# A depthwise convolution on TensorE and one product fewer on GpSimd, in a four-layer float32 network

## The chip, the cores and the metric

The kernel runs on one core of one Trainium2 chip, as one program. The metric is the device time of one execution in microseconds. The five engines are called here as in the profile: PE (TensorE, matrix products), DVE (VectorE), ACT (ScalarE), POOL or GpSimd, and SP, which issues most of the transfers. PSUM is the memory that PE writes its products to; DVE and ACT read it too; GpSimd works on SBUF alone in this kernel.

## What is computed

Four layers act on a tensor x of 8 samples, 384 channels and 32 x 32 pixels, in float32. The first and the third are state-space layers, the second a deformable convolution, the fourth a shift of channels by small separable kernels. The change is in the first, whose core is this (L = 1024 tokens, 768 inner channels, 16 states):

```python
x = x + mamba(group_norm(x))          # layer 0, on tokens
xz = xseq @ in_proj_w.T;  xin, z = split(xz)
xc = depthwise_conv(xin, conv_w, width 3, causal) + conv_b
u  = silu(xc)
dt, B, C = split(u @ x_proj_w.T);  dt = softplus(dt @ dt_proj_w.T + dt_proj_b)
h[t] = exp(dt[t] * A) * h[t-1] + dt[t] * u[t] * B[t]     # for each of 16 states
y[t] = sum over states of h[t] * C[t]  + u[t] * D
out  = (y * silu(z)) @ out_proj_w.T
```

The convolution of a channel is `w2*x[t] + w1*x[t-1] + w0*x[t-2] + b`.

## The kernel before

**Tiling.** `ssm_layer` is called for layer 0 and layer 2 with the same code and a few switches (`mlp` is true for layer 2). A sample's 1024 tokens are cut into two halves of 512 (`h` 0 and 1). One half of one sample is a *step*: 16 steps per layer, even ones first halves, odd ones second halves. The 768 inner channels are six groups `j` (or `d`) of 128. Within a group, the 128 channels x 16 states are laid out as eight *units* `m`, each a tile of 128 partitions x 2 x 512. So a step is 48 units, and one unit is:

- `inputs` (L502, GpSimd): `db = dub * B`, 128 x 1024, issued three units ahead;
- `decays` (L494, ACT): `da = exp(dtb * A)` in two operations, into PSUM, two units ahead; `da` has two buffers (`da0`, `da1`);
- `scan` (L514, DVE): the recurrence over 512 tokens, 128 x 1024;
- `with_c` (L525 on GpSimd, or L527 on DVE): the product with C, into `hs`, a ring of seven buffers;
- `keep_last` (L520, ACT), in first halves, and `add_carry` (L487, GpSimd) in second halves, which hand the state from one half to the next.

Every four units `read_out` (L537, PE) sums four `hs` tiles over the states into `y`. Which units have their product with C on GpSimd is told by `GP_C`: in layer 0 units 0, 2, 4, 6 of the even groups and 0, 2, 5 of the odd ones. For these the scan writes to `hs` itself; for the others it writes over `da`, and DVE makes the product right after it.

**Order.** Within the layer the order of each engine is written out by hand. `plan` puts all the rest of the work at unit numbers t (0 to 47) of a step, into one queue for each of ACT, DVE, GpSimd and PE. At unit t the loop does, in this order: ACT's queue for t, `scan`, `with_c` if it is DVE's, `keep_last`, `decays` of unit t+2, DVE's queue, `inputs` of unit t+3, `with_c` if it is GpSimd's, GpSimd's queue, PE's queue, `read_out`. Each engine executes its own instructions in the order in which they are issued.

The work of a step that is planned around the 48 units belongs to the step before (output projection), to the step itself (gate: z projection L546 on PE, then SiLU L550 on ACT between two table loads; softplus of dt, L408 to L451, for the group two ahead) and to the step after. For the step after, `inner` (L348) makes the input projection `ps_in` of group d at units `TI` = 15, 16, 17, 24, 25, 26 on PE, three products of 128 x 128 by 128 x 512 each; each float32 product is two PE instructions in the trace.

**The convolution before.** One unit after `inner`, `conv_last` (L352, ACT) writes `u = w2 * ps_in + b` to SBUF. In first halves it also copies the last two columns to `halo` (L354); in second halves it adds the two tokens that come from the half before, with three operations on single columns (L360). Two units after `inner`, `conv` (L368, DVE) adds the other two taps straight from PSUM, in two operations. Later SiLU runs over three groups at a time (L374). The first step's convolutions stand in a prologue that runs all groups in a row before the units begin.

PSUM tiles of PE's products (`ps_in`, `ps_dt`, `ps_sp`, `ps_z`, `ps_o`, `ps_x`) share three buffers; a new one takes a buffer whose readers are done.

Of the kernel before, what the change touches and what calls it, by code (L numbers as in the profile page):

```python
# [8 lines left out]
F32 = mybir.dt.float32  # L9
AF = mybir.ActivationFunctionType  # L10
ALU = mybir.AluOpType
# [4 lines left out]
P = 128  # L16
# [6 lines left out]
ND = DI // P  # L23
# [3 lines left out]
TS = L // 2  # L27
# [4 lines left out]
IP = P // NI  # L32
NSUB = P // IP
NQP = NS // NI // 2
GP_C = {0: ((0, 2, 4, 6), (0, 2, 5)), 2: ((0, 2, 5), (0, 2, 5))}
PE_SUM = (0,)
ENGINES = {mybir.EngineType.Activation, mybir.EngineType.PE, mybir.EngineType.DVE, mybir.EngineType.Pool}
FF = 4 * C
# [40 lines left out]
V_CW, V_CB, V_DB, V_D, V_A = 0, 18, 24, 30, 36  # L79
# [17 lines left out]
class Net:  # L97
# [107 lines left out]
    def ssm_layer(self, li, src, dst, shift=None):  # L205
        tc, nc, ins = self.tc, self.nc, self.ins
        mlp = li == 2
        gp_c = GP_C[li]
        pe_sum = li in PE_SUM
        sel = self.cols[:, Q_SEL : Q_SEL + IP]  # L210
        with ExitStack() as ctx:
            wp = ctx.enter_context(tc.tile_pool(name=f"w{li}", bufs=1))
# [11 lines left out]
            vec = wp.tile([P, ins[f"vec{li}"].shape[1]], F32, name="vec")  # L224
# [5 lines left out]
            if mlp:  # L230
                w1_d = ins["w1"].rearrange("(k p) o -> p k o", p=P)
                w2_d = ins["w2"].rearrange("(k p) o -> p k o", p=P)
                mean_w = wp.tile([P, P], F32, name="mean_w")
                nc.vector.memset(mean_w, 1.0 / C)
            else:
                win = wp.tile([P, G, 2 * DI], F32, name="win")
                nc.sync.dma_start(out=win, in_=win_d)
                wout = wp.tile([P, ND, C], F32, name="wout")
                nc.sync.dma_start(out=wout, in_=wout_d)
                diag_d = wp.tile([P, ND, P], F32, name="diag_d")  # L240
                for j in range(ND):
                    nc.gpsimd.tensor_scalar(
                        diag_d[:, j, :], self.ident, vec[:, V_D + j : V_D + j + 1], None, ALU.mult
                    )
            nc.sync.dma_start(out=wx, in_=ins[f"wx{li}"].rearrange("(k p) o -> p k o", p=P))
            nc.sync.dma_start(out=wdt, in_=ins[f"wdt{li}"])

# [8 lines left out]
            def v(i):  # L256
                return vec[:, i : i + 1]

            def fetch_in(s, o):
                if not mlp:  # L260
                    s["win", o] = win[:, :, o * P : (o + 1) * P]
                    return
                t = s["win", o] = p2.tile([P, G, P], F32, name="winr", tag="winr", bufs=3)
                nc.sync.dma_start(out=t, in_=win_d[:, :, o * P : (o + 1) * P])
# [75 lines left out]
            def inner(s, d):  # L340
                if d == 0:
                    s["u"] = p2.tile([P, ND, TS], F32, name="u", tag="u")
                    if s["h"] == 0:
                        s["sib"]["halo"] = p2.tile([P, ND, 2], F32, name="halo")
                xn, w = s["xn"], s["win", d]
                s["in", d] = ps = self.psum("ps_in")
                for k in range(G):
                    nc.tensor.matmul(ps, w[:, k, :], xn[:, k, :], start=(k == 0), stop=(k == G - 1))  # L348

            def conv_last(s, d):  # L350
                ps, ud = s["in", d], s["u"][:, d, :]
                nc.scalar.activation(ud, ps, AF.Identity, bias=v(V_CB + d), scale=v(V_CW + 3 * d + 2))  # L352
                if s["h"] == 0:
                    nc.scalar.copy(s["sib"]["halo"][:, d, :], ps[:, TS - 2 : TS])  # L354
                else:

                    halo = s["halo"][:, d, :]
                    for i, k, wi in ((0, 0, 0), (0, 1, 1), (1, 1, 0)):
                        c = ud[:, i : i + 1]
                        nc.scalar.activation(  # L360
                            c, halo[:, k : k + 1], AF.Identity, bias=c, scale=v(V_CW + 3 * d + wi)
                        )

            def conv(s, d):
                ps, ud = s["in", d], s["u"][:, d, :]
                w0, w1 = v(V_CW + 3 * d), v(V_CW + 3 * d + 1)
                for i, wi in ((1, w1), (2, w0)):
                    nc.vector.scalar_tensor_tensor(  # L368
                        ud[:, i:], ps[:, : TS - i], wi, ud[:, i:], ALU.mult, ALU.add
                    )  # L370
# [133 lines left out]
            def hs_tile(s, m):  # L504
                t = s["hs", m] = p2.tile([P, 2, TS], F32, name="hs", tag="hs", bufs=7)
                return t

            def scan(s, j, m):
                if j == 0 and m == 0 and s["h"] == 0:
                    s["sib"]["st"] = p2.tile([P, ND, NS], F32, name="st")  # L510
                da, db = s["da", m], s["db", m]
                h = hs_tile(s, m) if m in gp_c[j % 2] else da
                h1, da1, db1 = (t.rearrange("p i l -> p (i l)") for t in (h, da, db))
                nc.vector.tensor_tensor_scan(h1, da1, db1, 0.0, ALU.mult, ALU.add)  # L514
                s["h", m] = h
# [5 lines left out]

            def with_c(s, j, m):
                c = s["bc"][m // NSUB][:, 1]
                if m in gp_c[j % 2]:
                    nc.gpsimd.tensor_tensor(s["hs", m], s["hs", m], c, ALU.mult)  # L525
                else:
                    nc.vector.tensor_tensor(hs_tile(s, m), s["da", m], c, ALU.mult)  # L527
# [127 lines left out]
            def plan(prev, s, nxt):  # L655
                act, dve, pool, pe = queues = [[[] for _ in range(T + NU)] for _ in range(4)]

                def put(q, t, fn, *args):
                    if not args or args[0]:
                        q[t].append((fn, *args))  # L660

                for j in range(ND):
                    t = NU * j
# [6 lines left out]
                    n, k = (s, j + 2) if j + 2 < ND else (nxt, j + 2 - ND)  # L670
# [36 lines left out]
                for d, t in enumerate(TI):  # L707
                    put(pe, t - 2, fetch_in, nxt, d)
                    put(pe, t, inner, nxt, d)
                    put(act, t + 1, conv_last, nxt, d)  # L710
                    put(dve, t + 2, conv, nxt, d)
                put(pe, 32 if mlp else 30, x_proj, nxt, 0, ND // 2)
                put(pe, 33 if mlp else 32, x_proj, nxt, ND // 2, ND)
                put(act, 34 if mlp else 33, x_store, nxt)
# [32 lines left out]
            with tc.manual_schedule(engines=ENGINES):  # L747
                s = steps[0]
# [9 lines left out]
                for d in range(ND):  # L758
                    fetch_in(s, d)
                    inner(s, d)  # L760
                    conv_last(s, d)
                    conv(s, d)
                    if d == ND - 2:
                        silu(s, 0, ND // 2)
                x_proj(s, 0, ND // 2)
# [19 lines left out]
                for i, (s, j, m) in enumerate(units):  # L785
                    c, t = divmod(i, T)
                    if t == 0:
                        queues = plan(
                            steps[c - 1] if c else None, s, steps[c + 1] if c + 1 < len(steps) else None
                        )  # L790
                        for k, q in enumerate(over or ()):
                            for i0, items in enumerate(q):
                                queues[k][i0][:0] = items
                        act, dve, pool, pe = queues
                        over = [q[T:] for q in queues]
                    mine = m in gp_c[j % 2]
                    run(act[t])
                    scan(s, j, m)
                    if not mine:
                        with_c(s, j, m)  # L800
                    keep_last(s, j, m)
                    ahead = units[i + 2] if i + 2 < len(units) else (None, None, None)
                    if ahead[2] == 0:
                        first_token(*ahead[:2])
                    if ahead[0]:
                        decays(*ahead)
                    run(dve[t])
                    if i + 3 < len(units):
                        inputs(*units[i + 3])
                        if ahead[2] == 0:  # L810
                            carry(*ahead[:2])
                            add_carry(*ahead)
                        if units[i + 3][2] > 0:
                            add_carry(*units[i + 3])
                    if mine:
                        with_c(s, j, m)
                    run(pool[t])
                    run(pe[t])
                    for r in late.pop(i, ()):
                        read_out(*r)  # L820
                    if m % NSUB == NSUB - 1:
                        late.setdefault(i + (1 if m == NU - 1 else 2), []).append((s, j, m // NSUB))
# [1113 lines left out]
```

## Time and profile before

| | us |
|---|---|
| median of 3 runs | 9294.69 (9293.85 to 9295.26) |
| the profiled execution | 9297.33, span 9295.5 |
| layer 0: first to last scan, 16 steps | 75.5 to 2879.5 |
| an even step of layer 0 / an odd one | 172.1 / 179.5 |
| layers 1 / 2 and 3 | about 2900 to 5750 / from there to the end |

Mean durations in layer 0:

| operation | engine, line | us |
|---|---|---|
| scan, 128 x 1024 | DVE L514 | 2.29 |
| product with C, 128 x 1024 | DVE L527 / POOL L525 | 1.225 / 2.356 |
| `db`, 128 x 1024 | POOL L502 | 2.355 |
| decay, 128 x 512 | ACT L494 | 0.691 |
| `conv_last`, 128 x 512 | ACT L352 | 0.764 |
| single column | ACT L360 | 0.382 |
| tap of the convolution, 128 x 511 | DVE L368 | 0.745 |
| table load | ACT L550, L377 | 1.283 |

How to read the profile. A line of the *timeline* has the start in us from the first instruction, the duration in us, the engine, the source line, the operation, `out<-in`, sizes and the number of merged instructions; in brackets stands the idle time of the engine before it and what ended it by the profile. A line of the *groups* has the busy time in us, the mean in ns of one, and after the bar the idle time ahead of the group. A wait for several things is put down to one of them, and not always to the one that ended last. PE's matrix products overlap, so their durations are longer than their spacing. The clock column is the share of full speed that PE was granted.

### The profile page before, as it was taken

The page shows a single profiled execution, that of the slowest core. Times are in us where ns is not written, and L with a number is a line of the kernel's source. Part 1 is how long each engine was busy: PE and PEld are TensorE (multiplying, and loading weights), DVE is VectorE, ACT ScalarE, POOL GpSimd, SP SyncE. Part 2 cuts the span into 40 slices and gives each one's busy share as a digit, 9 for nine tenths or more (in the row PEclk, how much of TensorE's full clock was granted, in tenths as well). Part 3 has the DMA queues.
Part 4 walks back from the last instruction along what each step waited for, and adds up shares of the span by engine and source line. Part 5 has one row for each costly group of instructions (what it writes and reads, how often), then busy time and mean ns, then how long its engine had stood idle before and what let it go on. Part 6 is the DMA issues. An engine that isn't in the chain of part 4 may idle for free. (4 is left out here: it accounts for less than half of the span.)

```text
span 9295.5 us, 93074 instructions
## 1 busy us (share of the span) xinstructions
PE 7557.6 (81%) x29452; PEld 3856.6 (41%) x29452; DVE 7733.3 (83%) x8617; ACT 6500.3 (70%) x10467; POOL 5645.4 (61%) x3393
## 2 busy tenths in 40 slices
PE   6777677677676999999999997588888888888876
PEld 2222222222223777767777766133333333333333
DVE  6999999999995878878878877788988889898972
ACT  5677677677673878878877876677777677776750
POOL 6999999999994000000000000898989989899964
PEclk7788788788787999999999998798999889999988
DMA  4544544544543333333333333566656666666656
GB/s 123 124 115 113 123 116 114 123 119 114 123 114 81 82 80 85 92 83 85 90 84 86 91 80 85 118 154 151 150 139 155 151 161 147 148 148 145 161 145 112
DMA packets 785233, 1094.47 MB, mean 118 GB/s; under 512 B 274963, under 2 KB 427955, under 8 KB 752985
## 3 DMA queue, kind: packets, MB, share of 16 engines
q1 hardware_dynamic: 722628, 1077.98, 47.6%
q10 hardware_dynamic: 62100, 10.44, 0.7%
q8 instruction: 235, 3.85, 0.2%
q14 instruction: 270, 2.20, 0.1%
HBM read 917.84 MB, written 170.33 MB: 117 GB/s over the span
## 5 line engine op out<-in xcount | busy, mean ns | idle before, releaser
L502 POOL TENSOR_TENSOR db<-dub,bc 128x1024 f32<-128x1024 f32 x1536 | 3603.2, 2355 | 405.9 <-DVE hs L514 224.6
L494 ACT ACTIVATE da<-dtb,vec 128x512 f32<-128x512 f32 x3072 | 2119.5, 691 | 672.9 <-DVE hs L527 416.9
L514 DVE TENSOR_TENSOR_SCAN da<-da,db 128x1024 f32<-128x1024 f32 x912 | 2086.3, 2288 | 258.9 <-ACT da L494 116.4
L435 POOL TENSOR_TENSOR dt<-dt,sp_e 128x512 f32<-128x512 f32 x96 | 122.3, 1274 | 2885.4 <-DMA bc<-bcd 2881.1
L1598 PE MATMUL wacc<-fsm,fxk 128*128 128x221 f32 (+34 forms) x10624 | 1657.2, 315 | 98.1 <-DVE fsm L1568 95.1
L1598 PEld LDWEIGHTS wacc<-fsm,fxk 128*128 128x128 f32 x10624 | 1570.0, 195 | 236.1 <-DVE fsm L1568 159.2
L514 DVE TENSOR_TENSOR_SCAN hs<-da,db 128x1024 f32<-128x1024 f32 x624 | 1423.9, 2282 | 166.4 <-POOL db L487 76.7
L525 POOL TENSOR_TENSOR hs<-hs,bc 128x1024 f32<-128x1024 f32 x624 | 1470.8, 2357 | 15.2 <-ACT st L520 14.9
L1568 DVE TENSOR_TENSOR fsm<-fhy,fhx 128x170 f32<-128x170 f32 (+42 forms) x3216 | 1170.2, 428 | 342.3 <-PE wacc L1598 315.3
L527 DVE TENSOR_TENSOR hs<-da,bc 128x1024 f32<-128x1024 f32 x912 | 1116.9, 1225 | 111.8 <-PE y L537 58.5
L537 PE MATMUL y<-hs,cols 128*32 128x512 f32 x6144 | 826.1, 618 | 160.5 <-POOL hs L525 154.6
L1528 ACT ACTIVATE fhy<-fpyx,cell 128x416 f32<-128x416 f32 (+9 forms) x1280 | 645.5, 576 | 385.0 <-DVE fsm L1568 385.0
L1551 DVE TENSOR_TENSOR fxk<-fxt,fwk 128x1024 f32<-128x1024 f32 (+1 forms) x688 | 787.1, 1179 | 10.2 <-ACT fxt L1330 10.2
L614 PE MATMUL ps_m<-hid,wm 128*128 128x512 f32 x1152 | 550.2, 633 | 61.7 <-ACT hid L609 27.7
L595 PE MATMUL ps_h<-t,wm 128*128 128x512 f32 x1152 | 529.7, 604 | 43.2 <-DVE sp_e L427 25.4
L1533 ACT ACTIVATE fhy<-fhy,cols 128x1344 f32<-128x1344 f32 (+10 forms) x368 | 530.8, 1442 | 12.0
L537 PEld LDWEIGHTS y<-hs,cols 128*32 128x32 f32 x6144 | 171.3, 112 | 798.3 <-issue 497.7
L348 PE MATMUL ps_in<-xn,winr 128*128 128x512 f32 x576 | 328.9, 718 | 174.5 <-ACT xn L337 125.4
L444 PE MATMUL ps_sp<-dt,ident 128*128 128x512 f32 x192 | 168.4, 974 | 290.8 <-ACT dt L414 285.7
L614 PEld LDWEIGHTS ps_m<-hid,wm 128*128 128x128 f32 x1152 | 226.9, 203 | 394.3 <-issue 282.7
L1239 PE MATMUL ps_off<-fxn,fow 128*98 128x465 f32 (+10 forms) x896 | 386.6, 579 | 0.0
L444 PE MATMUL ps_sp<-sp_e,ident 128*128 128x512 f32 x192 | 174.9, 1009 | 259.5 <-DVE sp_e L425 259.5
(212 smaller groups left out, 10436.4 us busy)
## 6 DMA issues: line engine op xcount, KB each, us to landing
dtb<-dtd SPq DMA_DIRECT2D x768, 256.0 KB
dub<-dtd SPq DMA_DIRECT2D x768, 256.0 KB
fpyx<-fposd SPq DMA_DIRECT2D x640, 256.0 KB
wm<-in_w SPq DMA_DIRECT2D x96, 768.0 KB
bc<-bcd SPq DMA_DIRECT2D x256, 256.0 KB
x<-x SPq DMA_DIRECT2D x71, 768.0 KB
dtd<-dt SPq DMA_DIRECT2D x192, 256.0 KB
dtd<-sp_e SPq DMA_DIRECT2D x192, 256.0 KB
```

Of the source, the lines that this page charges most:

```text
L494: nc.scalar.activation(da[:, i, :], s["dtb", j][:, k, :], AF.Exp, scale=na[:, j, n + i : n + i + 1])
L502: nc.gpsimd.tensor_tensor(db, du, s["bc"][p][:, 0], ALU.mult)
L514: nc.vector.tensor_tensor_scan(h1, da1, db1, 0.0, ALU.mult, ALU.add)
L525: nc.gpsimd.tensor_tensor(s["hs", m], s["hs", m], c, ALU.mult)
L527: nc.vector.tensor_tensor(hs_tile(s, m), s["da", m], c, ALU.mult)
L537: nc.tensor.matmul(s["y"][k * IP : (k + 1) * IP, :], sel, s["hs", p * NSUB + k][:, i, :], start=mlp and p == 0 and i == 0, stop=p == NQP - ...
L614: nc.tensor.matmul(ps, s["w2", q][:, f, o * P : (o + 1) * P], s["hid", q][:, f, :], start=(f == 0), stop=(f == 3))
L1528: nc.scalar.activation(hy[:, at : at + (yb - ya) * W], pyx[:, 0, ya * W : yb * W], AF.Abs, bias=bias)
L1533: nc.scalar.activation(hy[:, :at], hy[:, :at], AF.Relu, bias=self.col(Q_ONE), scale=-1.0)
L1551: nc.vector.tensor_tensor(t[:, :n], x, wk[:, j : j + 1, :].to_broadcast([P, n, P]), ALU.mult)
L1568: nc.vector.tensor_tensor(self.sub(sm, at, [(r * w, n), (w, r), (1, w)]), self.sub(hy, hy_at[by] + xa, [(r * W, n), (W, r), (1, w)]), self ...
L1598: nc.tensor.matmul(a[:, ya - 4 * o : yb - 4 * o, xa:xb], k, self.sub(sm, sm_at[by], [(w, yb - ya), (1, w)]), start=False, stop=False,)
```

## The change

Three edits, all for layer 0. `GP_C` is now a list of six groups in both layers, with units 0, 2 and 5 in each; so in layer 0 the even groups give GpSimd three products in place of four, and DVE five in place of four. In a pair of groups GpSimd has six of sixteen products in place of seven. Layer 2 had this pattern before.

The convolution no longer uses DVE. `conv_in` copies the raw `ps_in` to SBUF. `conv_pe` multiplies it on PE by three diagonal matrices, shifted by 0, 1 and 2 columns, into a new PSUM tile `ps_cv`, with two small products for the two edge columns in second halves. `conv_out` adds the bias on the way back to SBUF. The diagonal matrices (18 of 128 x 128) are built once on GpSimd. Layer 2 keeps `conv_last` and `conv`.

```diff
-GP_C = {0: ((0, 2, 4, 6), (0, 2, 5)), 2: ((0, 2, 5), (0, 2, 5))}
+GP_C = {0: ((0, 2, 5),) * 6, 2: ((0, 2, 5),) * 6}
...
+                diag_w = wp.tile([P, 3 * ND, P], F32, name="diag_w")
+                for k in range(3 * ND):
+                    nc.gpsimd.tensor_scalar(
+                        diag_w[:, k, :], self.ident, vec[:, V_CW + k : V_CW + k + 1], None, ALU.mult
+                    )
...
+            def conv_in(s, d):
+                ps, ud = s["in", d], s["u"][:, d, :]
+                nc.scalar.copy(ud, ps)
+                if s["h"] == 0:
+                    nc.scalar.copy(s["sib"]["halo"][:, d, :], ps[:, TS - 2 : TS])
+
+            def conv_pe(s, d):
+                ud = s["u"][:, d, :]
+                s["cv", d] = ps = self.psum("ps_cv")
+                edge = s["h"] == 1
+                nc.tensor.matmul(ps, diag_w[:, 3 * d + 2, :], ud, start=True, stop=False)
+                nc.tensor.matmul(ps[:, 1:], diag_w[:, 3 * d + 1, :], ud[:, : TS - 1], start=False, stop=False)
+                if edge:
+                    halo = s["halo"][:, d, :]
+                    nc.tensor.matmul(ps[:, 0:1], diag_w[:, 3 * d + 1, :], halo[:, 1:2], start=False, stop=False)
+                    nc.tensor.matmul(ps[:, 0:2], diag_w[:, 3 * d, :], halo, start=False, stop=False)
+                nc.tensor.matmul(ps[:, 2:], diag_w[:, 3 * d, :], ud[:, : TS - 2], start=False, stop=True)
+
+            def conv_out(s, d):
+                nc.scalar.activation(s["u"][:, d, :], s["cv", d], AF.Identity, bias=v(V_CB + d))
...
-                h = hs_tile(s, m) if m in gp_c[j % 2] else da
+                h = hs_tile(s, m) if m in gp_c[j] else da
...
-                    put(act, t + 1, conv_last, nxt, d)
-                    put(dve, t + 2, conv, nxt, d)
+                    if mlp:
+                        put(act, t + 1, conv_last, nxt, d)
+                        put(dve, t + 2, conv, nxt, d)
+                    else:
+                        put(act, t + 1, conv_in, nxt, d)
+                        put(pe, t + 1, conv_pe, nxt, d)
+                        put(act, t + 3, conv_out, nxt, d)
...
-                    conv_last(s, d)
-                    conv(s, d)
+                    for fn in (conv_last, conv) if mlp else (conv_in, conv_pe, conv_out):
+                        fn(s, d)
```

The last hunk is the prologue of the first step. The same change of index, from `gp_c[j % 2]` to `gp_c[j]`, is made at two other places.

## The prediction

> **What bounds the kernel now.** The change touches the first state-space layer only, so I read that layer. The page first: five engines, none full over the span. Then the table of stretches, cut at two neighbouring steps of the layer (a step is 48 units, and a unit is one scan). Columns: PE, PEld, DVE, ACT and POOL busy, then granted clock, DMA share, GB/s.
>
> ```profile
> PE 7557.6 (81%) x29452; PEld 3856.6 (41%) x29452; DVE 7733.3 (83%) x8617; ACT 6500.3 (70%) x10467; POOL 5645.4 (61%) x3393
> ```
> ```profile
> 1132.80:1304.90 172.10, 126.54 (x374) 41.46 (x370) 160.13 (x109) 128.27 (x236) 162.11 (x73) 0.81 0.49 118
> 1304.90:1484.40 179.50, 131.04 (x415) 47.39 (x418) 164.44 (x120) 123.31 (x203) 167.33 (x121) 0.81 0.48 118
> ```
>
> The layer is 16 such steps: even ones (first half of a sample) 172.1 us, odd ones 179.5. DVE and GpSimd are both busy some 93% of a step, and PE 73%. The change takes work from the two full engines and gives it to PE, so the question is what DVE waits for in the remaining 7%. The timeline of the even step, DVE, then ACT, then PE, where the convolutions stand:
>
> ```profile
> 1186.84 2.28 DVE L514 TENSOR_TENSOR_SCAN hs<-da,db 128x1024 f32<-128x1024 f32 x1
> 1190.54 2.30 DVE L514 TENSOR_TENSOR_SCAN da<-da,db 128x1024 f32<-128x1024 f32 x1 [1.42 <-POOL db L502]
> ```
> ```profile
> 1186.93 0.60 ACT L550 ACTIVATE sz<-ps_z 128x512 f32<-128x512 f32 x1 [1.60 <-PE ps_z L546]
> 1187.55 1.28 ACT L377 ACT_TABLE_LOAD   x1
> ...
> 1189.04 1.42 ACT L494 ACTIVATE da<-dtb,vec 128x512 f32<-128x512 f32 x2
> 1190.39 0.76 ACT L352 ACTIVATE u<-ps_in,vec 128x512 f32<-128x512 f32 x1
> ```
> ```profile
> 1186.73 5.31 PE L348 MATMUL ps_in<-xn,win 128*128 128x512 f32 x12
> 1191.98 1.93 PE L537 MATMUL y<-hs,cols 128*32 128x512 f32 x16
> 1193.83 2.84 PE L348 MATMUL ps_in<-xn,win 128*128 128x512 f32 x6
> ```
>
> DVE idles 1.42 us before the scan at 1190.54. The row names GpSimd, but the last thing to end before it is ACT's `da` (1189.04 + 1.42 = 1190.46), and ACT was late because its gate waited 1.60 us for PE's `ps_z`. So in this stretch the order is PE, then ACT, then DVE: ACT executes in order, its decays `da` of unit u+2 stand behind whatever the plan put at unit u, and what waits there for PE holds the next scan. One row shows what PE does after a long wait:
>
> ```profile
> 1229.82 5.42 PE L348 MATMUL ps_in<-xn,win 128*128 128x512 f32 x6 [4.75 <-DVE u L368]
> ```
>
> **The parts of the change, each by itself.**
>
> ```profile
> L527 DVE TENSOR_TENSOR hs<-da,bc 128x1024 f32<-128x1024 f32 x432 | 529.1, 1225 | 32.2 <-PE y L537 5.1 <-DVE da L514 0.5
> L368 DVE SCALAR_TENSOR_TENSOR u<-ps_in,vec,u 128x511 f32<-128x511 f32 x192 | 143.0, 745 | 17.4 <-ACT halo L354 14.0
> L525 POOL TENSOR_TENSOR hs<-hs,bc 128x1024 f32<-128x1024 f32 x336 | 791.6, 2356 | 1.2 <-ACT st L520 0.9
> ```
>
> - DVE, per step: 12 `conv` operations go (12 x 0.745 = 8.94 us), three products with C come (3 x 1.225 = 3.68). Net -5.27.
> - GpSimd: three products go, 3 x 2.356 = 7.07 us per step. It hides behind DVE except in odd steps, where `add_carry` (L487) makes it the later one at three or four units.
> - ACT, per convolution: `conv_last` (0.76) becomes a copy (taken as 0.60, from L447's 0.58) and `conv_out` (taken as 0.76, as L352). Where the next step is a second half, three L360 operations of 0.38 go. About even in time; what counts is that ACT now waits twice on PE's queue.
> - PE, per convolution: three float32 products, which the trace before has with `win` as weights, not with a diagonal. A product 128x512 is two instructions; six took 2.84 us in the row at 1193.83 and 5.42 in the row at 1229.82. These are the ends; I take 2.6, the spacing at full clock (2.84 less the drain of the last), since PE is busy just ahead of most convolutions. In even steps, whose successor is a second half, two edge products of one and two columns come on top: nothing at the low end, L145's 18 instructions of 128x2 in 4.00 us at the other, 4 x 0.21 = 0.85, which I take.
> - SP's queue gets no transfer. `spread` of dt and du leaves up to 5 us later where PE's sums come later; its tiles are first used seven units on, some 23 us: nothing.
> - 18 diagonal matrices in the prologue on GpSimd: 18 x 0.58 (`diag_d`: 6 in 3.50 us) = 10.5, finished near 19 us, before the first convolution at 28. Nothing.
>
> **What they do to the path, by hand.** PE's queue now reads in0, conv0, in1, readout, conv1, in2, dt, conv2 and later in3, readout, conv3, in4, dt, conv4, in5, conv5. Each conv waits for ACT's copy of its `in`, and everything behind waits too. I walked the even step with the durations above. An instruction starts when its engine is free and what it reads has ended, in the order of the queues: ACT does, for each unit, first what the plan put there (copies, conv_out, soft_exp, gate), then `keep_last`, then `da` of two units on (1.42). DVE's scan takes 2.2 and a product with C 1.2 from start to start. Zero is 1175.86 us, the start of the scan of unit 13.
>
> | event | before | after |
> |---|---|---|
> | in0 ends (PE) | 13.6 | 13.6 |
> | ACT has taken in0 (behind `da` of 17, 14.6) | 15.3 | 15.15 |
> | conv0: waits 1.6 for that, then 2.6 + 0.85 | - | 18.7 |
> | in1 ends | 16.2 | 21.4 |
> | copy of in1, then `da` of 19 ends (ACT) | 21.1 | 23.5 |
> | scan 19 | 23.9 | 23.5 |
> | readout (1.9) and conv1 (3.45) end | 18.0 | 26.55 |
> | in2 ends | 20.8 | 29.3 |
> | copy of in2, then `da` of 20 ends | 24.3 | 31.5 |
> | scan 20 (DVE was free at 26.95) | 28.8 | 31.5 |
> | scan 21 (behind soft_exp 2.6 and conv_out on ACT) | 31.6 | 36.5 |
> | scan 25 (behind gate and two table loads) | 46.0 | 50.75 |
> | conv3 52.9 to 56.35; in4 ends | 50.8 | 59.1 |
> | in5: behind soft_exp and `conv_out` of conv3, whose PSUM buffer it takes | 59.2 | 67.4 |
> | scan 29 (DVE free at 65.35) | 64.1 | 69.6 |
> | scan 33 | 78.7 | 84.4 |
>
> DVE idles some 13 us more here and works 7.7 us less: the even step is 5.7 us longer. Outside this stretch the extra product of j = 0 and j = 4 (1.2 us) falls into bubbles ahead of units 9 and 41 that ACT's gate makes anyway (1.3 and 1.8 us): nothing.
>
> Odd steps have no edge products. The same walk gives scan 25 at +1.7 and scan 33 at +2.2 us; against it some 2 us of DVE's waits for GpSimd go (list of waits: DVE for L487 43.7 + 35.4 us over eight odd steps, near 10 a step, of which I take only those at units 40 to 46 and 8, since the others sit where ACT is late anyway). Near 0.
>
> Prologue: before, PE runs the 36 `ps_in` instructions without a gap (22.44 to 40.3) and `dbc` is there at 48.1. After, each of six channels is in (2.6), wait for the copy (0.85), conv (2.6) in a row, 6.05 instead of 2.57 us, and the last three go through conv_out and SiLU afterwards: my chain ends at 67.6, +19.5, with nothing beside it.
>
> **Sum:** 8 even steps x 5.7 = 46; 7 odd ones x 0.2 = 1; the last step, which plans no successor, -1; prologue +19.5. Together +66 us. The profiled execution took 9297.33 us (span 9295.5), 2.6 above the median of 9294.69; the difference carries over to the median: 9361.
>
> The Trainium skill, "TensorE: Matmul & The Clock Gate", section "Part 1: The HAM clock gate", says that PE falls to half clock after an idle window of about 3.4 us. The row at 1229.82 agrees: six instructions took 5.42 us after a wait of 4.75, against 2.84. By that rule the waits of my walk (1.6, 2.7 and 1.4 us) would leave PE at full clock, and the sum stands.
>
> **The rivals.**
> 1. *Faster: PE keeps up.* If the copy of in2 came back so early that `da` of 20 were done when DVE is free (26.95, so 4.55 us sooner than in my walk, and likewise 4.25 at scan 29), DVE alone would decide: -5.27 x 15 steps = -79, +19.5 for the prologue: 9235. For it: both full engines lose work, and DVE's list of waits names GpSimd first. Against: the bubble at 1190.54 shows ACT and PE as the late ones already. If all waits on GpSimd went too (43.7 + 39.3 + 35.4 + 15.6 + 3.3 = 137 us in DVE's list), 9100; that is the far end.
> 2. *Slower still: PE goes cold, or the readouts come too late.* conv0, conv3 and in5 each start after a wait; at the rate of the row at 1229.82 each costs 2.6 more: 8 us a step, 15 steps, 120 us: 9481; half of it 9420. The same sign has the `hs` ring of seven: in my walk the readouts end 1 us before DVE needs the buffers.
> 3. *No change.* ACT's waits cost half as much as walked: the steps give back what the prologue costs, 9290 to 9310.
> 4. That the change doesn't do what it says I exclude: no convolution of this layer stands on DVE any more.
>
> **Numbers.** Forecast 9361 (own range 9320 to 9400): 0.52. Rival 2: 0.20. Rival 3: 0.12. Rival 1: 0.16. A measurement of this kernel tells about 0.2% (19 us) from no change. Faster 0.15, same 0.12, slower 0.73. The range leaves out the far ends of rivals 1 and 2: 9225 to 9470.
>
> **What would show it.** In the profile after: DVE idle before scans 20 and 29 of every step, with ACT's `da` ending last; ACT's copies waiting for `ps_in`; even steps near 178 us, odd ones near 180; the first scan near 95 us instead of 75.5. It would be wrong if DVE's idle time per step did not grow (then rival 1), or if the six instructions of a convolution took 5 us (rival 2).

## The result and the profile after

The changed kernel takes 9395.6 us (9393.93 to 9398.12, four runs), the kernel before beside it 9294.27 (9288.03 to 9295.26): 1.0108 of the time before, 95% interval 1.0096 to 1.012. The forecast of 9361 had the sign, and the range of 9225 to 9470 holds the time (its own narrower range, 9320 to 9400, only just), but 35 of the 101 us were not in the sum. The profiled execution has a span of 9392.6 us, 97.1 more than before; all but 1.5 of it stands in the first state-space layer.

The page's first line, busy time by engine, answers to the line of the page before:

```profile
PE 7695.8 (82%) x30195; PEld 3951.1 (42%) x30220; DVE 7662.7 (82%) x8473; ACT 6484.7 (69%) x10419; POOL 5553.4 (59%) x3363
```

DVE lost 71 us of work and GpSimd 92, PE gained 138; and the kernel is slower. The table of stretches, cut at the same two steps (columns: PE, PEld, DVE, ACT and POOL busy, then granted clock, DMA share, GB/s), shows where it went:

```profile
1178.50:1358.70 180.20, 136.20 (x433) 48.30 (x425) 155.87 (x101) 125.41 (x225) 154.70 (x70) 0.86 0.46 113
1358.70:1542.10 183.40, 138.81 (x445) 51.97 (x444) 160.26 (x112) 123.94 (x207) 162.99 (x119) 0.85 0.47 115
```

DVE works 4.3 us less in the even step (155.87 against 160.13), and the step is 8.1 us longer. So it idles 12 us more. DVE and GpSimd are both busy 86% of the step now (93 and 94% before), and PE, with its new work, 76% (74% before): it is still idle a quarter of the step. This points to order, not to capacity; an experiment below decides it. DVE's list of waits over this layer names the new releaser (total us, times, longest):

```profile
DVE da L540 <- ACT da L520: 113.4, 59, 3.7
DVE da L540 <- issue: 65.8, 35, 3.8
DVE hs L540 <- ACT da L520: 63.2, 30, 3.9
DVE u L583 <- PE y L563: 33.8, 15, 2.5
```

Before, the list was led by GpSimd:

```profile
DVE hs L514 <- POOL db L487: 43.7, 34, 3.7
```

Now ACT's decays lead, by name. The timeline shows why. DVE first; zero of the walk, the scan of unit 13, is 1223.39 here:

```profile
1241.63 2.28 DVE L540 TENSOR_TENSOR_SCAN hs<-da,db 128x1024 f32<-128x1024 f32 x1
1246.37 0.69 DVE L583 TENSOR_TENSOR u<-y,sz 128x512 f32<-128x512 f32 x1 [2.46 <-PE y L563]
1254.19 2.30 DVE L540 TENSOR_TENSOR_SCAN da<-da,db 128x1024 f32<-128x1024 f32 x1 [3.67 <-ACT da L520]
```

Then ACT: the copies of the raw projection (L357) wait for PE, and the decays (L520) stand behind them:

```profile
1244.45 0.59 ACT L357 COPY u<-ps_in 128x512 f32<-128x512 f32 x1 [4.54 <-PE ps_in L353]
...
1252.10 0.59 ACT L357 COPY u<-ps_in 128x512 f32<-128x512 f32 x1 [4.94 <-PE ps_in L353]
...
1252.67 1.42 ACT L520 ACTIVATE da<-dtb,vec 128x512 f32<-128x512 f32 x2
```

And PE, whose next projection (L353) stands behind the convolution (L365 to L371), which stands behind ACT's copy:

```profile
1238.56 1.13 PE L365 MATMUL ps_cv<-u,diag_w 128*128 128x512 f32 x2 [1.55 <-ACT u L357]
1239.52 1.02 PE L366 MATMUL ps_cv<-u,diag_w 128*128 128x511 f32 x2
1240.38 0.28 PE L369 MATMUL ps_cv<-halo,diag_w 128*128 128x1 f32 x2
1240.52 0.36 PE L370 MATMUL ps_cv<-halo,diag_w 128*128 128x2 f32 x2
1240.74 1.10 PE L371 MATMUL ps_cv<-u,diag_w 128*128 128x510 f32 x2
1241.68 2.74 PE L353 MATMUL ps_in<-xn,win 128*128 128x512 f32 x6
```

The reader is to see one loop through two queues: copy, convolution, next projection, next copy. In this stretch ACT waits 4.5 to 5 us of each round (2.5 and 2.9 us in the second stretch, at units 25 to 29), and the scan waits for the decay behind the copy. PE itself waits less: 1.55 us here, 2.49 us before the first convolution of the second stretch. One wait is of another kind: at 1246.37 DVE had waited 2.46 us for PE's readout, which stands behind the same projection.

### The profile page after: what moved, and what is told of

Read it like the earlier page. It is cut to its first block, busy times and chain, and to the rows that moved or that the text cites. A ratio compares the mean times of both kernels' runs of the same rounds, so it can differ in the third digit from the quotient of the medians.

```text
span 9392.6 us, 94371 instructions
## 1 busy us (share of the span) xinstructions
PE 7695.8 (82%) x30195; PEld 3951.1 (42%) x30220; DVE 7662.7 (82%) x8473; ACT 6484.7 (69%) x10419; POOL 5553.4 (59%) x3363
## 5 line engine op out<-in xcount | busy, mean ns | idle before, releaser
L520 ACT ACTIVATE da<-dtb,vec 128x512 f32<-128x512 f32 x3072 | 2119.4, 691 | 597.9 <-DVE hs L553 390.5
L540 DVE TENSOR_TENSOR_SCAN da<-da,db 128x1024 f32<-128x1024 f32 x960 | 2196.2, 2288 | 333.7 <-ACT da L520 196.7
L540 DVE TENSOR_TENSOR_SCAN hs<-da,db 128x1024 f32<-128x1024 f32 x576 | 1315.2, 2283 | 200.8 <-ACT da L520 110.6
L551 POOL TENSOR_TENSOR hs<-hs,bc 128x1024 f32<-128x1024 f32 x576 | 1359.4, 2360 | 79.9 <-ACT st L546 79.7
L553 DVE TENSOR_TENSOR hs<-da,bc 128x1024 f32<-128x1024 f32 x960 | 1175.7, 1225 | 107.0 <-PE y L563 50.7
L563 PE MATMUL y<-hs,cols 128*32 128x512 f32 x6144 | 782.5, 610 | 104.2 <-POOL hs L551 98.2
L353 PE MATMUL ps_in<-xn,winr 128*128 128x512 f32 x576 | 332.8, 725 | 171.7 <-ACT xn L342 125.7
L1546 ACT ACTIVATE fhx<-fpyx,cell 128x544 f32<-128x544 f32 (+8 forms) x640 | 380.1, 667 | 0.0
```

The costliest lines, as they stand in the source:

```text
L520: nc.scalar.activation(da[:, i, :], s["dtb", j][:, k, :], AF.Exp, scale=na[:, j, n + i : n + i + 1])
L563: nc.tensor.matmul(s["y"][k * IP : (k + 1) * IP, :], sel, s["hs", p * NSUB + k][:, i, :], start=mlp and p == 0 and i == 0, stop=p == NQP - ...
```

## The walk beside the trace

The same events in this even step, from 1223.39 on:

| event | walked | measured |
|---|---|---|
| conv0 starts / in1 ends | 15.2 / 21.4 | 15.2 / 21.0 |
| `da` of 19 ends / scan 19 | 23.5 / 23.5 | 23.2 / 23.6 |
| in2 ends | 29.3 | 28.7 |
| scan 20 | 31.5 | 30.8 |
| scan 25 | 50.75 | 51.3 |
| in5 ends | 67.4 | 67.0 |
| scan 29 | 69.6 | 69.3 |
| scan 33 | 84.4 | 84.1 |

Scan 19 came at the walked time by another way: its `da` was there at 23.2, but DVE still had the close (L583) to do, which had waited for the readout. The walk did not have that wait.

And the whole layer, from the starts of the scans in both traces, in groups of eight units (j = 0 to 5):

| term | forecast, us | measured, us |
|---|---|---|
| prologue (first scan 75.5 to 95.3) | +19.5 | +19.8 |
| even steps, j = 2, 3 (the walked stretch) | +46 | +38.7 |
| even steps, j = 0, 1, 4, 5 | 0 | +23.2 |
| seven odd steps | +1 | +19.8 |
| last step | -1 | -6.0 |
| after the layer | 0 | +1.5 |
| sum | +66 | +97.1 |

So the walk of the convolution holds for even steps, and so does the prologue. Two terms that were called nothing make 43 us. The experiments had to settle both: whether the convolution costs what was walked, and what the product with C costs.

## The experiments

**Theories.** *Order* (the forecast's): the convolution on PE is slow because everything behind it in PE's queue waits for ACT's copy. *Capacity*: PE has too much work for its granted clock. *Product*: the product with C that moved to DVE does the harm, by its number or by its place. First the parts of the change, each alone.

**Convolution alone.** The change with the products of before:

```diff
-GP_C = {0: ((0, 2, 5),) * 6, ...
+GP_C = {0: ((0, 2, 4, 6), (0, 2, 5)) * 3, ...
```

> The convolution goes to TensorE as in the changed kernel; the products with C stay as before (units 0, 2, 4, 6 of the even groups on GpSimd). Chain theory (what costs is that TensorE's queue and ScalarE's queue wait for each other in the stretch of the convolutions): the stretch from scan 17 to scan 33 stays long, groups 0 and 4 of the even steps go back from 26.8 and 28.6 to 25.1 and 27.1 us, the first scan stays at 95.3; about 9360. Product theory (the three products that came to VectorE are the cost): even steps go back to 172 or below, and with the convolution off VectorE the kernel is at most 9294 plus the 20 us of the prologue.

Measured: 9370.51 us (9369.82 to 9373.93), 1.0081 of before, interval 1.0064 to 1.0097. By the ends of the layer's scans it is 77 us: prologue 21.9, j = 2 and 3 of even steps 42.8 (5.4 a step, 5.7 walked), j = 0, 1, 4 and 5 of even steps 3.7, odd steps 8.7. The convolution is slower by itself, and where the walk said. (In four of the eight even steps PE also ran slow for one convolution; this is taken up under the rivals below.)

**Products alone.** The kernel before with the products of the change:

```diff
-GP_C = {0: ((0, 2, 4, 6), (0, 2, 5)), ...
+GP_C = {0: ((0, 2, 5), (0, 2, 5)), ...
```

> The kernel before with only the products moved (units 0, 2, 5 of every group on GpSimd); the convolution stays on VectorE. Chain theory: within 25 us of before, even steps about 3 us longer through groups 0 and 4, odd steps and the last step shorter where GpSimd was late (last step 162 instead of 168), together 9270 to 9300. Product theory: at or above 9370.

Measured: 9339.32 us (9332.76 to 9342.19), 1.0046 of before, interval 1.0029 to 1.0063: a miss. Half of the change that was expected to cost nothing costs 45 us. Even steps are 5.5 us longer, odd ones 1.2, the last one 6.2 shorter. The two parts alone add up to more (77 + 44 by the ends of the layer) than the change has (96): the waits of the one cover a part of the other's.

**Prologue back on DVE.** The change, with the first step's convolutions as before:

```diff
-                    for fn in (conv_last, conv) if mlp else (conv_in, conv_pe, conv_out):
+                    for fn in (conv_last, conv):
```

> The changed kernel, but the six convolutions of the prologue are made as before (ScalarE and VectorE); all later ones stay on TensorE. If the prologue's chain of copy, product, copy costs what the first scan shows (95.3 instead of 75.5), this is 9395.6 - 19.8 = 9376, and the steps are as in the changed kernel. If its delay would be swallowed later, it stays at 9395.

Measured: 9377.74 us (9376.03 to 9383.11), ratio 1.009 (1.0073 to 1.0107). The first scan is back at 77.1 us, 18.3 us earlier, and the kernel is 17.9 us faster. So the total gives back the prologue's delay. The trace does not show it step by step: at the end of the layer 11 us of it are left, and 6 appear behind the layer, a part that has the same code in all runs and still varies between them by more than that (6411 to 6427 us).

**The same work, later in PE's queue.** The three products stand two units later, so that `inner` of the next groups goes ahead of them:

```diff
-                        put(pe, t + 1, conv_pe, nxt, d)
-                        put(act, t + 3, conv_out, nxt, d)
+                        put(pe, t + 3, conv_pe, nxt, d)
+                        put(act, t + 4, conv_out, nxt, d)
```

> The changed kernel with the same instructions in another order: the convolution's products stand three units after the input projection instead of one, the copy out four instead of three, so that TensorE makes all three input projections of a stretch before the first convolution and waits for no copy. Chain theory: ScalarE no longer waits for the projections, the idle time of VectorE before scans 18, 20, 25 and 29 (about 12 us of a step) falls to what it was before the change (2 to 4 us); even steps 168 to 173, odd ones 170 to 175, the kernel 9220 to 9290. TensorE-capacity theory (TensorE has 18 products more in a step, and its clock is what limits): no change from 9395, or at least 9360.

Measured: 9260.35 us (9254.22 to 9261.77), ratio 0.9961 (0.9947 to 0.9975), 135 us faster than the change with the same instructions on every engine. The stretch of an even step, columns as above:

```profile
1131.20:1302.20 171.00, 133.83 (x437) 48.45 (x440) 155.44 (x101) 125.89 (x226) 154.18 (x70) 0.86 0.50 119
```

PE's busy time and granted clock are those of the change (133.8 and 136.2 us, 0.86 and 0.86); the step is 9.2 us shorter. That ends the capacity theory. PE's timeline of this run, at the units that were shown above:

```profile
1187.56 5.31 PE L353 MATMUL ps_in<-xn,win 128*128 128x512 f32 x12
1192.81 1.92 PE L563 MATMUL y<-hs,cols 128*32 128x512 f32 x16
1194.66 2.84 PE L353 MATMUL ps_in<-xn,win 128*128 128x512 f32 x6
1197.43 1.12 PE L434 MATMUL ps_dt<-dbc,wdt 24*128 24x512 f32 x2
1198.48 1.12 PE L365 MATMUL ps_cv<-u,diag_w 128*128 128x512 f32 x2
```

and ACT's:

```profile
1193.14 0.58 ACT L357 COPY u<-ps_in 128x512 f32<-128x512 f32 x1
...
1197.54 0.59 ACT L357 COPY u<-ps_in 128x512 f32<-128x512 f32 x1 [0.90 <-PE ps_in L353]
```

The three projections run ahead, and ACT's copies wait 0 and 0.90 us in place of 4.54 and 4.94. DVE's idle time before the scans of units 20 and 29 is gone, and so is that before the close (L583), between the scans of units 18 and 19.

**One tap in place of three.** The change with only the product for `w2`; the other two taps and the edge columns are left out of the convolution:

```diff
                 nc.tensor.matmul(ps, diag_w[:, 3 * d + 2, :], ud, start=True, stop=True)
```

> The changed kernel in its order, but each convolution on TensorE has one product only (the tap of the token itself; the other two taps and the edge products are left out), so its time in the queue falls from 2.6 or 3.4 us to 0.9, while both waits (TensorE for the copy, ScalarE for the projection behind it) stay. If the length of the products that stand ahead of the next projection is the price, VectorE's idle time before scans 18, 20 and 29 falls by most of its 10 us, even steps to 171 to 174 and the kernel to 9280 to 9310. If the round trip between the two queues is the price whatever its products last, steps stay within 3 us and the kernel above 9350.

Measured: 9300.14 us (9292.33 to 9314.42), ratio 1.0005 (0.9995 to 1.0015). Of the 95 us that this saves, 10 lie in the prologue. Even steps are 175.0 us, 5.2 less than in the change and still 2.9 over before. So the length of what stands ahead of the next projection makes most of the price of an even step. As for the rest, the products with C are where the change has them, so it isn't the convolution's alone.

**Both remedies**: the late convolution, and the prologue on DVE.

> The late order of the convolution together with the prologue as before. If the two effects add, 9260 - 18 = 9242, steps as with the late order alone.

Measured: 9244.6 us (9241.47 to 9249.2), ratio 0.9946 (0.993 to 0.9963).

**Both remedies with the products of before** (`((0, 2, 4, 6), (0, 2, 5)) * 3`):

> The late order, the prologue as before, and the products with C as before (units 0, 2, 4, 6 of even groups on GpSimd). VectorE has 3.7 us less in each step than with the moved products, GpSimd 7.1 more. If VectorE is what bounds the even steps, these fall from 171 to about 167.5; GpSimd then bounds the odd ones (175 to 177) and the last step returns to 168; together 9225 to 9245, no worse than with the products moved. If the move of the products is worth what it takes off GpSimd, it is slower, 9260 or more.

Measured: 9220.22 us (9217.5 to 9231.67), ratio 0.9919 (0.9903 to 0.9936), faster than expected. The moved product costs 24 us here too. It isn't its number, as the next two runs show.

**Both remedies, the product of another unit moved.** Even groups give GpSimd units 0, 2 and 4 in place of 0, 2 and 5: the same counts, but the extra product on DVE is that of unit 6, where before had it on GpSimd, and units 4 and 5 stay as they were.

> The late order, the prologue as before, and three products of even groups on GpSimd as in the change, but units 0, 2 and 4 in place of 0, 2 and 5; so VectorE's extra product stands at unit 6, just ahead of ScalarE's gate, and not at unit 4. If only the number of products counts, the time equals that of units 0, 2, 5 (about 9242). If the place counts, because an extra product at unit 6 falls into the idle time that the gate makes at units 9, 25 and 41, even groups get up to 1.2 us shorter, and in odd steps GpSimd has no product just ahead of the state that it carries over (VectorE waits 2.5 us for it at unit 8): 9200 to 9225.

Measured: 9214.67 us (9213.48 to 9217.98), ratio 0.9914 (0.9897 to 0.993), 30 us less than with 0, 2, 5.

**Products alone, units 0, 2, 4.** The kernel before with `((0, 2, 4), (0, 2, 5))`; the convolution is untouched.

> The kernel before, convolution untouched, with C products on GpSimd 0,2,4 in even groups and 0,2,5 in odd ones (VectorE has one more product per step, as in the products-alone run, but at unit 6 of the later stretch, and the fifth product as before on VectorE). If the place of the extra VectorE product in the step's chain is what cost the products-alone run its 45 us: 9275 to 9300, even steps 172 to 174. If the mere number of products on VectorE costs it: about 9339 again, even steps 177 to 178.

Measured: 9287.41 us (9281.4 to 9290.38), ratio 0.9992 (0.9982 to 1.0002): no change, where 0, 2, 5 had cost 45 us, with the same instructions on each engine. (In sum over the layer the even steps are 9 us longer than before, the odd ones 10 and the last one 7 shorter.) The trace tells how. Products alone with 0, 2, 5, even step, units 36 to 41; DVE, PE and ACT in turn:

```profile
1287.27 1.22 DVE L527 TENSOR_TENSOR hs<-da,bc 128x1024 f32<-128x1024 f32 x1
1288.41 0.68 DVE L425 SCALAR_TENSOR_TENSOR sp_e<-sp_w,ps_dt 128x512 f32<-128x512 f32 x1
...
1303.05 2.30 DVE L514 TENSOR_TENSOR_SCAN da<-da,db 128x1024 f32<-128x1024 f32 x1 [1.99 <-issue]
```
```profile
1289.14 2.08 PE L444 MATMUL ps_sp<-sp_e,ident 128*128 128x512 f32 x2 [3.88 <-DVE sp_e L425]
...
1296.57 2.84 PE L546 MATMUL ps_z<-xn,win 128*128 128x512 f32 x6
```
```profile
1299.45 0.60 ACT L550 ACTIVATE sz<-ps_z 128x512 f32<-128x512 f32 x1 [1.57 <-PE ps_z L546]
```

The same with 0, 2, 4:

```profile
1264.85 2.28 DVE L514 TENSOR_TENSOR_SCAN hs<-da,db 128x1024 f32<-128x1024 f32 x1
1267.05 0.66 DVE L425 SCALAR_TENSOR_TENSOR sp_e<-sp_w,ps_dt 128x512 f32<-128x512 f32 x1
...
1281.40 2.30 DVE L514 TENSOR_TENSOR_SCAN da<-da,db 128x1024 f32<-128x1024 f32 x1 [0.43 <-issue]
```
```profile
1267.77 2.08 PE L444 MATMUL ps_sp<-sp_e,ident 128*128 128x512 f32 x2 [2.60 <-DVE sp_e L425]
```
```profile
1277.79 0.60 ACT L550 ACTIVATE sz<-ps_z 128x512 f32<-128x512 f32 x1
```

In unit 4 of each group DVE has the softplus's `sp_e` (L425), and from it hangs a chain: PE's sums (L444), behind them in PE's queue the readout and the gate's z projection (L546), ACT's gate (L550), the decay behind it, and the second scan of the next group (here unit 41). With 0, 2, 5 the product of unit 4 stands on DVE ahead of `sp_e`. The whole chain moves by its 1.2 us, and the wait at its end moves along instead of shrinking. With 0, 2, 4 the extra product comes at unit 6, behind `sp_e`: the chain stays where it is, and DVE has work to do while it waits. The gate then starts without a wait. PE's part of the chain is shorter here too, 9.7 us from the start of `sp_e` to the end of the z projection against 10.8 before and 11.0 with 0, 2, 5; but ACT's table load ends only at 1277.78, so with 10.8 the gate would have started some 0.1 us later (an estimate from these rows). Means over six even steps of DVE's idle time before the scans of units 9, 25 and 41: before 1.3, 2.3 and 1.8 us; 0, 2, 5: 1.7, 3.2 and 1.9; 0, 2, 4: 0.4, 1.8 and 0.6. The two patterns differ by 4.0 us in these three waits, and by 4.2 in the even step (177.6 and 173.4).

**Both remedies, 0, 2, 4 in all six groups.**

> The best version so far (readouts two units later, prologue's convolution taken back to VectorE, products 0,2,4 in even groups, 0,2,5 in odd ones: 9214.7) with 0,2,4 in the odd groups too. If the place of GpSimd's last product ahead of its carry and decay sums delays the odd groups also: 9195 to 9212, odd steps 170 to 171. If only even groups were hurt by it: 9212 to 9218 and odd steps unchanged at 172. If odd groups were better with 0,2,5: above 9218.

Measured: 9188.47 us (9184.58 to 9188.51), ratio 0.9886 (0.9869 to 0.9902), the fastest of all, a little below the range given. Its two steps:

```profile
1091.20:1258.60 167.40, 134.61 (x440) 48.69 (x436) 155.42 (x101) 125.17 (x226) 154.81 (x71) 0.88 0.51 122
1258.60:1429.10 170.50, 136.39 (x452) 52.31 (x445) 159.65 (x113) 124.57 (x208) 161.30 (x117) 0.86 0.51 124
```

DVE's work is that of the changed kernel within 0.7 us (155.4 against 155.9, 159.7 against 160.3), and the steps are 13 us shorter. The even steps lose the 1.4 us that they had before unit 17, behind a group that had 0, 2, 5.

**The changed kernel itself with 0, 2, 4 in even groups** (convolution and prologue as in the change):

> The change itself, with GpSimd's products at units 0,2,4 in the even groups in place of 0,2,5 (same counts on both engines; convolution and prologue as in the change). If the prediction's step on the extra product failed for the unit it stands at, the steps shed what groups 0 and 4 cost (23 us over the layer) and a part of the odd steps' excess: 9345 to 9380. If it failed because one more product on VectorE is one more on the path: 9396 again.

Measured: 9359.8 us (9358.95 to 9365.6), ratio 1.007 (1.0054 to 1.0087). Of the layer's terms, j = 0, 1, 4 and 5 of the even steps go from +23.2 to +7.0 us, the odd steps from +19.8 to +5.7; the walked stretch stays (+38.7 and +40.5). So the place of these products made the change 36 us slower, and what is left over before is 65 us, beside a forecast of 66. That the two are so close is partly luck: the walked stretch is some 6 us smaller than forecast and the last step's gain some 6 us larger, and the terms that were called nothing make up for it.

**The changed kernel with 0, 2, 4 in all groups.**

> The change with 0,2,4 in all six groups. With the late convolution this took 26 us off. If the same holds beside the early convolution: 9320 to 9360. If the waits of the early convolution cover it: as the run with 0,2,4 in even groups, within 10 us.

Measured: 9361.66 us (9358.55 to 9365.75), ratio 1.007 (1.0053 to 1.0086): nothing more. The wait before unit 17 goes here too (1.43 to 0.14 us), but even steps are hardly shorter (177.8 against 178.2): units 28 and 29, in the stretch of the early convolution, wait 2.7 us longer. PE's rate has a part in that. The first convolution of the second stretch now waits some 3.5 us where it had waited 2.49, and its ten instructions, 3.28 us at full rate, take 4.9 to 6.0 us in seven of the eight even steps (in one of eight in the run before):

```profile
1627.57 1.12 PE L365 MATMUL ps_cv<-u,diag_w 128*128 128x512 f32 x2 [3.49 <-ACT u L357]
...
1632.34 2.77 PE L353 MATMUL ps_in<-xn,win 128*128 128x512 f32 x6
```

The granted clock was 0.55 from 1628.6 to 1632.3. In the eighth even step the same convolution ran at full rate after the same wait; there groups 2 and 3 took 67.4 us and the step 176.2, against 69.1 to 69.4 and 177.6 to 178.0 in the settled others. So much of the gain ahead of this stretch went into a slower PE.

## Why the prediction was right, and where it fell short

1. **"DVE idles some 13 us more here and works 7.7 us less: the even step is 5.7 us longer."** Right, in mechanism and nearly in size: +38.7 us over the layer, 5.2 in the step shown (62.9 to 68.1 for j = 2 and 3), 5.4 with the convolution alone; and the loop copy, convolution, projection is shown by moving it: two units later takes 135 us off. DVE idles before scans 20 and 29 with `da` last, as said.
2. **"my chain ends at 67.6, +19.5, with nothing beside it."** Right: +19.8, and 18 us came back when this part alone was undone.
3. **"Outside this stretch the extra product of j = 0 and j = 4 (1.2 us) falls into bubbles ahead of units 9 and 41 that ACT's gate makes anyway (1.3 and 1.8 us): nothing."** This step failed: 23 us. The bubbles are real and can take a product, but only one that stands behind the operation from which the bubble's chain starts. The pattern 0, 2, 5 doesn't only take unit 6 from GpSimd: it trades unit 4 for unit 5, and unit 4 is ahead of `sp_e`. The prediction counted the products (five for four) and didn't ask at which unit they stand. With 0, 2, 4 the step would have been nearly right: +3.7 us over the layer in j = 0, 1, 4 and 5 of the products alone, and in the change +7.0.
4. **"7 odd ones x 0.2 = 1"** failed as well: +19.8. The walked stretch was undersized (+2.2 a step; 21.9 / 7 = 3.1). One reason is PE's rate. In all seven odd steps that plan a successor the first convolution of the second stretch ran slow, and not after a long wait:

```profile
1459.08 1.70 PE L365 MATMUL ps_cv<-u,diag_w 128*128 128x512 f32 x2 [2.21 <-ACT halo L359]
1460.58 1.91 PE L366 MATMUL ps_cv<-u,diag_w 128*128 128x511 f32 x2
...
1463.45 2.74 PE L353 MATMUL ps_in<-xn,win 128*128 128x512 f32 x6
```

   Its six instructions took 4.5 us in place of 2.8; the granted clock was 0.56 from 1459.1 to 1462.3, and 1.00 from 1467.2 to 1470.0. With the convolution alone it ran slow in four odd steps and at full rate in three: groups 2 and 3 took 64.4 to 65.6 us in the former, 62.9 to 63.4 in the latter. So this is worth some 1.5 us of the stretch, about 10 us over seven steps (an estimate: no run had the change's own odd steps with PE at full rate). And of "some 2 us of DVE's waits for GpSimd" those at units 40 to 46 did go (3.1 us a step before, 0.9 after, at unit 41), but the one at unit 8 grew from 1.1 to 2.4 us. GpSimd and then DVE in the changed kernel, units 4 to 8 of the odd step:

```profile
1385.27 2.37 POOL L528 TENSOR_TENSOR db<-dub,bc 128x1024 f32<-128x1024 f32 x1 [4.32 <-DMA dub<-dtd]
1387.60 2.35 POOL L551 TENSOR_TENSOR hs<-hs,bc 128x1024 f32<-128x1024 f32 x1
1389.92 2.33 POOL L528 TENSOR_TENSOR db<-dub,bc 128x1024 f32<-128x1024 f32 x1
1392.23 0.21 POOL L503 TENSOR_TENSOR a<-a,st 128x16 f32<-128x16 f32 x1
1392.52 0.34 POOL L513 TENSOR_TENSOR db<-db,a 128x2 f32<-128x2 f32 x2
```
```profile
1392.74 2.29 DVE L540 TENSOR_TENSOR_SCAN hs<-da,db 128x1024 f32<-128x1024 f32 x1 [2.60 <-POOL db L513]
```

   The same in the run with both remedies and 0, 2, 4:

```profile
1288.52 2.35 POOL L551 TENSOR_TENSOR hs<-hs,bc 128x1024 f32<-128x1024 f32 x1
1293.02 4.69 POOL L528 TENSOR_TENSOR db<-dub,bc 128x1024 f32<-128x1024 f32 x2 [2.15 <-DMA dub<-dtd]
1297.67 0.21 POOL L503 TENSOR_TENSOR a<-a,st 128x16 f32<-128x16 f32 x1
```
```profile
1298.19 2.29 DVE L540 TENSOR_TENSOR_SCAN hs<-da,db 128x1024 f32<-128x1024 f32 x1 [0.42 <-POOL db L513]
```

   With 0, 2, 4 GpSimd makes its product while it waits for the transfer of `dub`. With 0, 2, 5 it waits 4.32 us idle, and the product of unit 5 comes after, ahead of the carry (L503) that the scan of unit 8 needs: 6.96 us from the transfer to the carry, against 4.65. One product, 2.35 us, on the wrong side of a wait.
5. **"the last step, which plans no successor, -1"**: -6.0 in the change, -6.2 with the products alone, +0.2 with the convolution alone. Without a convolution beside it GpSimd was the late engine there (busy 164.1 of the step's 168.2 us before), and its seventh product was worth more than the sum had.
6. **Rival 1, "PE keeps up"**, was wrong for this order and right for another: with the late convolution PE keeps up, and the kernel is faster than before. **Rival 2**, a cold PE, did not come in the walked even step: the convolution at 1238.56 after a wait of 1.55 us took 3.12 us to the next projection, and in5, 5.42 us before, now takes 2.84 after a wait of 0.89. But it came in part: one convolution in each of seven odd steps (item 4) and in one of the eight even ones (4.96 us in place of 3.28) ran slow, and with the late convolution none did. The other half of this rival, late readouts, is there too, 2.46 us in each settled even step at the close; scan 19 came on time all the same. The Trainium skill, "TensorE: Matmul & The Clock Gate", section "Part 1: The HAM clock gate", puts the fall to half clock at an idle window of about 3.4 us. The traces agree above that (5.42 us for six instructions after a wait of 4.75) but not below: a wait of 2.21 us was enough in the odd steps, while after 2.49 us seven of eight even steps kept full rate. So of the waits of 1.6, 2.7 and 1.4 us that the prediction took as harmless by this rule, the middle one (measured 2.49 us in even steps, 2.21 in odd ones) was not always harmless.

**What stays open.** What the last 2.9 us of the even step are in the run with one tap was not separated; it has the products at 0, 2, 5, and the two weren't parted there. Why the two parts together cost 96 us and not 121 is only argued: the products alone lengthen j = 2 and 3 of even steps by 15.9 us, and in the change this lies beside the convolution's waits. Why PE fell to the lower clock after 2.21 us in the odd steps and mostly kept the full one after 2.49 us in the even ones is open; the length of the wait alone does not tell.

## What to carry to other kernels

Where engines work through queues in a fixed order, an operation that goes to another engine takes its place in that queue with it: ask what stands behind it, and whether the other engine's answer is in time for that; here the same products of the convolution, two units later, took 135 us off. A bubble takes in extra work only from behind the point where its chain begins; look for that point (the last operation of the waiting engine that the chain reads) and count units, not totals. A wait put ahead of a matrix product can also slow the product itself: look at PE's granted clock behind each new wait. And before a wait on a transfer is a good place for work, after it a bad one.

## What the runs showed of the hardware

The edge products of one and two columns were taken at 0.85 us; by the starts of the rows they cost 0.36 (1240.38 to 1240.74), so a whole convolution with edges is 3.12 us from start to start, not 3.45. The mean granted clock of an even step was 0.81 before and 0.86 in the changed kernel, and PE's busy time in an even step rose by only 9.7 us (126.54 to 136.20) for six convolutions that take 6 x 3.12 = 18.7 from start to start. So the work that PE had before became some 9 us shorter (117.4 us without the convolutions): in5 alone 2.6 us, where it comes after a wait of 0.89 us in place of 4.75. And the clock could fall after a wait of 2.21 us (item 4): six instructions took 4.5 us in place of 2.8.
